# Second attention's first unit placed beside the last shared units of the first feed-forward

## The chip, the core and the metric

The kernel runs on one core of one Trainium2 chip. A core has five engines with a queue of instructions each: PE (TensorE, matrix products; its weight loads are listed as PEld), DVE (VectorE), ACT (ScalarE), POOL (GpSimd) and SP (SyncE, which here issues DMAs). Each engine takes its own instructions strictly in the order of its queue, and engines wait for each other by semaphores. The metric is the device time of one execution in microseconds (us).

## The reference

Two layers in float32 on x of 4 x 1024 rows of 256 numbers, that is 32 row tiles of 128 rows (NT = 32):

```
x = x + windowed_attention(layernorm(x))       # 16 heads, window 64
x = x + moe(layernorm(x))                      # first feed-forward
x = x + attention(layernorm(x))                # 16 heads over all keys, then a layernorm
x = x + expert_choice(layernorm(x))            # second feed-forward, sinkhorn gates
```

The first feed-forward has eight routed experts, of which each row uses its best two, and two shared experts whose mean every row gets. An expert is silu(x w1 + b1) * (x w2 + b2), times w3, plus b3, with 512 hidden columns. In the second attention 64 rows of 256 numbers are reread as the 1024 positions of one head (the reference reshapes to (B * H, S, D) without a transpose), so that a unit of rows can be attended to without the others. The second feed-forward takes sinkhorn gates and lets each expert choose 128 of 1024 rows.

## The kernel before

The rows lie in SBUF for the whole kernel, as tiles x_t[0] to x_t[31]. Four tiles make a unit (UT = 4, NU = 8). A scheduler in the language keeps the order in which instructions are written as a start, reorders each engine's queue by its own estimates, and puts in the waits that data and reuse of memory ask for. Pools hand out SBUF; a tile that takes over memory of an earlier one waits for that one's last reader.

*First feed-forward.* normalise writes the normed rows xn_kept of each tile and their transposes xnT. The gate chooses two experts for each row; 64 scatters (L840, one for each tile and choice, on POOL) write rows to xs_d in DRAM sorted by expert. Beside them run the shared experts: shared(E, u) for all eight units, then shared(E + 1, u) for u = 0 and 1. One shared(e, u) is 32 matmuls of 128x512 at L657, a Silu at L665 on ACT and a product at L666 on DVE for each of four groups f, then 32 matmuls at L674 and four updates of x_t at L683. Then 31 blocks of sorted rows go through their experts (L876 transposes, L893 and L920 matmuls), with expert weights from a pool f0_e of three buffers, and their results are written to ys_d. After the blocks the second shared expert's weights are loaded again (load_expert) and shared(E + 1, u) runs for u = 2 to 7. After these in the program come 64 gathers (L947, indirect DMAs on POOL, three buffers yr0): each fetches the rows of one tile and one choice from ys_d, and DVE adds them, weighted, to x_t[i] (L953). note(i) then takes mean and variance of tile i on DVE (L137, L138); roots takes the square root on ACT and the reciprocal on DVE (L143, L144).

*Constants of the second feed-forward* follow (L965 to L1000): two iotas, the zero fill of rank_d and of the last row of y_d by six DMAs on POOL.

*Second attention.* Weights and biases are loaded (w_raw, b_raw on SP; bv_b and rows_b on POOL), two top_st tiles and minus are filled by memsets on POOL (L1308 to L1313). project(u) makes, for a unit, normed rows xn (L1325, on POOL), their transposes (L1335), q and k (L1345 matmuls, L1356 and L1357 split them in two parts) and writes these to DRAM as halves. load(p) reads them back as q_st and k_st, the stack for head pair group p, into a ring of RING stacks. values(u) makes v_t. maxima_step computes scores once (L1423 on PE, two matmuls) and their row maxima (L1430 on DVE). AHEAD = 12 steps of these, two halves each, are issued before the main loop; the loop of NP * KT + 1 = 257 steps then, for each step, computes scores less the row maximum (L1465), exponentials (L1473 on ACT), sums with v (L1480), and the maxima 12 steps ahead. Between them some() runs small jobs, twice a step: generators that yield when they have given enough work for one turn. put_out (L1513 to L1526) adds the bias bo on POOL (L1525) and the projection on DVE; finish makes the last norm on POOL (L1553 to L1558).

*Ranks.* When the first half of the batch has been gated, the generator ranks() issues 16 scatters on POOL (L1591) that write a row's place to rank_d; it yields 0 after each, so that they may all be issued in one turn. choose_steps later reads rank_d and makes key.

Of the kernel before, what the change touches and what calls it, by code (L numbers as in the profile page):

```python
# [18 lines left out]
P = 128  # L19
# [10 lines left out]
E = 8  # L30
# [9 lines left out]
def two_layers(  # L40
# [464 lines left out]

    with ExitStack() as lc:  # L510
        wpool = lc.enter_context(tc.tile_pool(name="f0_w", bufs=1))
        epool = lc.enter_context(tc.tile_pool(name="f0_e", bufs=3))
        pool = lc.enter_context(tc.tile_pool(name="f0", bufs=2))
        xnT = wpool.tile([P, 2, NT * P], F32, name="xnT_f0")
        dram = lc.enter_context(tc.tile_pool(name="f0_d", bufs=1, space=bass.MemoryType.DRAM))
# [21 lines left out]
        for k in range(2):  # L537
            t = pool.tile([P, D], F32, tag="yr0", name="sb3_k", bufs=3)
            nc.gpsimd.dma_start(out=t, in_=sb3[k].partition_broadcast(P))
            if k == 0:  # L540
                nc.gpsimd.tensor_scalar(sb3_b, t, 0.5, None, ALU.mult)
            else:
                nc.gpsimd.tensor_scalar(t, t, 0.5, None, ALU.mult)
                nc.gpsimd.tensor_tensor(sb3_b, sb3_b, t, ALU.add)
# [90 lines left out]
        def kept_rows(i: int):  # L635
            xn_all.append(wpool.tile([P, D], F32, name=f"xn_kept{i}"))
            return xn_all[i]

        def load_expert(w1, w2, w3):
# [8 lines left out]
        def shared(e: int, weights, u: int):  # L648
# [3 lines left out]
            glu = pool.tile([P, NF, UN], F32, tag="glu", name="glu")  # L652
            for f in range(NF):
# [10 lines left out]
                act = pool.tile([P, UN], F32, tag="act", name="act", bufs=3)  # L664
# [3 lines left out]
                )  # L668
            for jp in range(UT // 2):
# [11 lines left out]
                for jj in range(2):  # L681
# [8 lines left out]
                    )  # L690

# [6 lines left out]
        first = load_expert(sw1[0], sw2[0], sw3[0])  # L698
# [154 lines left out]
        second = load_expert(sw1[1], sw2[1], sw3[1])  # L853
# [3 lines left out]

        for t0, nt, n in order:
# [4 lines left out]
                *(w[bass.ds(e, 1)].rearrange("e k f -> (e k) f") for w in (rw1, rw2, rw3))  # L863
            )
            b3_t = pool.tile([P, 1, D], F32, tag="b3", name="b3_t")
# [3 lines left out]
            xb = pool.tile([P, 2, D], F32, tag="xb", name="xb", bufs=2)  # L869
# [11 lines left out]
            xbT = pool.tile([P, 2, BT], F32, tag="xbT", name="xbT")  # L881
# [45 lines left out]
            yb = pool.tile([P, 2, D], F32, tag="yb", name="yb")  # L927
# [11 lines left out]
        second = load_expert(sw1[1], sw2[1], sw3[1])  # L939
        for u in range(2, NU):  # L940
            shared(E + 1, second, u)


        for i in range(NT):
            for k in range(2):
                yr = pool.tile([P, D], F32, tag="yr0", name="yr0", bufs=3)
                nc.gpsimd.indirect_dma_start(  # L947
                    out=yr[:, :],
                    out_offset=None,
                    in_=ys_d[:, :],  # L950
                    in_offset=bass.IndirectOffsetOnAxis(ap=slots[k][:, i : i + 1], axis=0),
                )
                nc.vector.scalar_tensor_tensor(  # L953
                    x_t[i], yr, weight[k][:, i, :], x_t[i], ALU.mult, ALU.add
                )
            note(i)

    fc = ctx.enter_context(ExitStack())
    fpool = fc.enter_context(tc.tile_pool(name="f1_w", bufs=1))
    gpool = fc.enter_context(tc.tile_pool(name="f1", bufs=2))
    fdram = fc.enter_context(tc.tile_pool(name="f1_d", bufs=1, space=bass.MemoryType.DRAM))
    GB = 2  # L965
    GE = GB * E
    TB = S // P
    GT = GB * TB

    gw1 = fpool.tile([P, 2, E], F32, name="gw1")  # L970
    nc.sync.dma_start(out=gw1, in_=gate1_w.rearrange("(k p) e -> p k e", p=P))

    number_i = fpool.tile([P, E], I32, name="number_i")
    nc.gpsimd.iota(number_i, pattern=[[1, E]], base=0, channel_multiplier=0)
    number = fpool.tile([P, 1, E], F32, name="number")
    nc.vector.tensor_copy(number[:, 0, :], number_i)
    first_slot = fpool.tile([P, 1, E], F32, name="first_slot")
    nc.vector.tensor_scalar(first_slot, number, float(CAP), -1.0, ALU.mult, ALU.add)

    place1_i = fpool.tile([P, 1], I32, name="place1_i")  # L980
    nc.gpsimd.iota(place1_i, pattern=[[0, 1]], base=1, channel_multiplier=1)
    place1 = fpool.tile([P, 1], F32, name="place1")
    nc.vector.tensor_copy(place1, place1_i)
    gates = fpool.tile([P, NT, E], F32, name="gates")

    xn_d = [fdram.tile([S, D], F32, name=f"xn_d{b}") for b in range(NB)]

    y_d = [fdram.tile([E * CAP + 1, D], F32, name=f"y_d{b}") for b in range(NB)]

    rank_d = [fdram.tile([S * E, 1], F32, name=f"rank_d{b}") for b in range(GB)]  # L990
    none = fpool.tile([P, S * E // P], F32, name="none")
    nc.gpsimd.memset(none, 0.0)
    for b in range(GB):
        nc.gpsimd.dma_start(out=rank_d[b].rearrange("(p n) o -> p (n o)", p=P), in_=none)
    for b in range(NB):
        nc.gpsimd.dma_start(
# [790 lines left out]
```

## Time and profile before

| | us |
|---|---|
| median of 3 runs | 2609.26 |
| lowest, highest | 2599.96, 2613.25 |
| time of the profiled execution | 2548.45 |
| its span in the profile | 2546.3 |
| mean granted clock of PE in it | 0.94 |
| last block's last matmul (L920) | 1144.8 |
| last shared unit ends on PE | 1275.4 |
| last gather starts | 1278.8 |
| first maxima matmul (L1423) | 1317.5 |
| first exponential (L1473) | 1354.8 |
| 16 rank scatters (L1591) | 2309.2 to 2329.2 |

The profile is of one execution. Its rows give for each engine the busy time; times of day are us from the start of the span. "PEclk" is the share of its full clock that PE was granted. A row of waits says which engine and instruction waited for which: us in total, how often, the longest. "A to B" rows give busy us of each engine in that stretch with the number of instructions in brackets. The median of the runs is 2.4% above the profiled execution; parts of the time are read in the profiled execution.

### The profile page before, as it was taken

What the parts mean: (1) busy time and instruction counts of PE and PEld (TensorE: products, weight loads), DVE (VectorE), ACT (ScalarE), POOL (GpSimd) and SP (SyncE); (2) the same over time, 40 slices, a digit from 0 to 9 for tenths busy, and PEclk for the clock granted to TensorE, in tenths of its full rate; (3) what the DMA queues carried; (4) which work ended last, traced back from release to release, by engine and by line L of the source; (5) the groups of instructions that cost most, each with busy time, mean ns of one, the idle gap of its engine ahead of it and who ended that gap; (6) DMA issues with size and microseconds to landing.
All of it is one profiled execution on the core that took longest, in us unless ns stands there. A gap on an engine that the chain in (4) does not pass through costs nothing. (4 is left out here: it accounts for less than half of the span.)

```text
span 2546.3 us, 42216 instructions
## 1 busy us (share of the span) xinstructions
PE 2291.9 (90%) x16844; PEld 1361.5 (53%) x16844; DVE 1398.2 (55%) x2294; ACT 980.1 (38%) x1350; POOL 639.7 (25%) x742
## 2 busy tenths in 40 slices
PE   6999999799999999998948999999999999997534
PEld 3666666566578888885524444444444444443322
DVE  6445445524322222225446777677777898984293
ACT  1333333312112222221103666565666565665311
POOL 2333333510710000005330021212222212124355
PEclk8988999899999999999968999999999999998667
DMA  3000000320346667652152121213121312100134
GB/s 93 18 10 10 11 12 10 125 77 3 131 160 212 205 206 230 206 172 75 50 118 68 35 68 44 68 44 68 44 68 43 68 44 67 44 19 11 54 120 132
DMA packets 201535, 206.46 MB, mean 81 GB/s; under 512 B 89224, under 2 KB 161544, under 8 KB 201340
## 3 DMA queue, kind: packets, MB, share of 16 engines
q1 hardware_dynamic: 178732, 163.24, 22.4%
q0 software_dynamic: 11792, 30.18, 4.0%
q10 hardware_dynamic: 10816, 10.36, 1.2%
q8 instruction: 133, 2.18, 0.4%
q14 instruction: 62, 0.51, 0.1%
HBM read 142.28 MB, written 56.96 MB: 78 GB/s over the span
## 5 line engine op out<-in xcount | busy, mean ns | idle before, releaser
L1430 DVE TENSOR_REDUCE tops<-two 128x2 f32<-128x1024 f32 x512 | 619.4, 1218 | 128.1 <-PE two L1423 126.0
L1473 ACT ACTIVATE pT<-two 128x1024 f32<-128x1024 f32 x512 | 523.0, 1024 | 331.3 <-PE two L1465 326.6
L1480 PE MATMUL acc<-pT,v_t 128*32 128x256 f32 x4096 | 346.3, 398 | 5.3 <-ACT pT L1473 5.3
L1465 PE MATMUL two<-q_st,k_st 64*128 64x512 f32 x1024 | 262.0, 504 | 31.8 <-DVE tops L1430 19.5
L893 PE MATMUL two<-xbT,w_t 128*128 128x256 f32 (+1 forms) x1280 | 257.9, 356 | 1.3 <-ACT xbT L882 0.7
L1423 PE MATMUL two<-k_st,q_st 64*128 64x512 f32 x1024 | 233.2, 422 | 20.2 <-DMA k_st<-halves 9.4
L893 PEld LDWEIGHTS two<-xbT,w_t 128*128 128x128 f32 x1280 | 222.7, 190 | 31.1 <-ACT xbT L882 5.1
L657 PE MATMUL two<-xnT_f,w_t 128*128 128x512 f32 x512 | 230.4, 601 | 5.6 <-DVE glu L666 5.6
L1465 PEld LDWEIGHTS two<-q_st,k_st 64*128 64x128 f32 x1024 | 97.4, 185 | 224.8 <-issue 128.2
L1465 PE MATMUL two<-top_st,minus 64*128 64x512 f32 x1024 | 209.2, 402 | 0.0
L909 DVE SCALAR_TENSOR_TENSOR glu_b<-two,b_blk,act_b 128x256 f32<-128x256 f32 (+1 forms) x160 | 72.6, 454 | 228.7 <-ACT act_b L903 228.7
L903 ACT ACTIVATE act_b<-two,b_blk 128x256 f32<-128x256 f32 (+1 forms) x160 | 71.9, 450 | 310.9 <-PE two L893 159.5
L947 POOL DMA_INDIRECT yr<-ys_d,slot x64 | 61.2, 956 | 499.5 <-DMA ys_d<-yb 433.0
L1480 PEld LDWEIGHTS acc<-pT,v_t 128*32 128x32 f32 x4096 | 87.0, 109 | 169.6 <-issue 147.7
L657 PEld LDWEIGHTS two<-xnT_f,w_t 128*128 128x128 f32 x512 | 96.4, 193 | 114.1 <-issue 105.8
L1423 PEld LDWEIGHTS two<-k_st,q_st 64*128 64x128 f32 x1024 | 108.1, 192 | 92.2 <-DVE tops L1430 28.8
L920 PE MATMUL acc<-w_t,glu_b 128*128 128x256 f32 x568 | 148.5, 390 | 8.3 <-DVE glu_b L909 4.0
L355 DVE TENSOR_REDUCE top<-two 128x4 f32<-128x768 f32 (+1 forms) x128 | 112.5, 919 | 69.4 <-PE two L329 69.4
L381 POOL TENSOR_SCALAR_AFFINE_SELECT pT<-pT 128x1024 f32<-128x1024 f32 x64 | 70.2, 1097 | 305.8 <-ACT pT L378 300.4
L378 ACT ACTIVATE pT<-two 128x768 f32<-128x768 f32 (+1 forms) x128 | 93.7, 783 | 123.0 <-PE two L329 122.6
L665 ACT ACTIVATE act<-two,bT 128x512 f32<-128x512 f32 x64 | 44.0, 687 | 242.2 <-PE two L657 239.5
L1525 POOL TENSOR_TENSOR y<-y,rows_b 128x256 f32<-128x256 f32 x32 | 23.4, 733 | 431.6 <-DVE y L1522 431.6
(320 smaller groups left out, 3185.1 us busy)
## 6 DMA issues: line engine op xcount, KB each, us to landing
w_t<-in_L_ffn_rw_dram SPq DMA_DIRECT2D x120, 512.0 KB
halves<-split SPq DMA_DIRECT2D x64, 256.0 KB
q_st<-halves SPq DMA_DIRECT2D x128, 128.0 KB
k_st<-halves SPq DMA_DIRECT2D x256, 64.0 KB
xb<-xs_d SPq DMA_DIRECT2D x31, 256.0 KB
ys_d<-yb ACTq DMA_DIRECT2D x31, 256.0 KB
xs_d<-zeros SPq DMA_DIRECT2D x5, 1536.0 KB
b_t<-in_L_ffn_rb_dram SPq DMA_DIRECT2D x40, 128.0 KB
```

Source lines behind the costliest of these rows:

```text
L355: nc.vector.tensor_reduce(tops[i][:, 2 * ab : 2 * ab + 2, 2 * gp : 2 * gp + 2], scs[ab], AX.X, ALU.max)
L378: nc.scalar.activation(pt[:, 2 * ab : 2 * ab + 2, :, :n], scs[ab], AF.Exp)
L657: mm(ps[:, n * 512 : (n + 1) * 512], lhsT=w_t[:, kc, f * P : (f + 1) * P], rhs=xnT[:, kc, cols], start=(kc == 0), stop=(kc == 1),)
L893: mm(ps[:, m * 512 + ff * cols : m * 512 + (ff + 1) * cols], lhsT=w_t[:, kc, f * P : (f + 1) * P], rhs=xbT[:, kc, :cols], start=(kc == 0), ...
L903: nc.scalar.activation(act[:, :cols], ps[:, ff * cols : (ff + 1) * cols], AF.Silu, bias=b_blk[0][:, f, n : n + 1],)
L909: nc.vector.scalar_tensor_tensor(glu[:, f, :cols], ps[:, 512 + ff * cols : 512 + (ff + 1) * cols], b_blk[1][:, f, n : n + 1], act[:, :cols ...
L920: mm(ps[:, a * D : (a + 1) * D], lhsT=glu[:, f, a * P : (a + 1) * P], rhs=w3_t[:, f, :], start=(f == 0), stop=(f == NF - 1),)
L1423: mm(sc[:, hh], lhsT=q_st[rows, j * P : (j + 1) * P], rhs=k_st[rows, kk * 512 : (kk + 1) * 512], start=True, stop=True,)
L1430: newest["vector"] = nc.vector.tensor_reduce(tops[:, :, j, kk], sc, AX.X, ALU.max).ins
L1465: mm(sc[:, hh * 512 : (hh + 1) * 512], lhsT=minus[rows] if top else k_st[rows, k * P : (k + 1) * P], rhs=(top_ring[p % 2] if top else q_st ...
L1473: newest["scalar"] = nc.scalar.activation(pt, sc, AF.Exp).ins
L1480: newest["tensor"] = mm(oT_ps[32 * r : 32 * r + 32, hh * D : (hh + 1) * D], lhsT=vals[n // HU][:, n % HU, k, :], rhs=pts[r // 2][:, hh * 5 ...
```

## The change

1. The pool and the constants of the second feed-forward (L965 to L1000, with the zero fill of rank_d and y_d, and ones1) are written ahead of the first feed-forward. The constant number of that stage is called expert_no.
2. The shared experts' weights get a pool of their own, f0_s, with two buffers; the second is loaded once. xn_kept lies in a pool f0_k that is closed before the blocks; the pools of the blocks, f0_e and f0_b, take memory from there on. The gathers have seven buffers (yr0) in place of three.
3. What the second attention needs for its first unit (weights, two stacks of q and k, one top_st, minus, xnT, split) is taken from the other end of SBUF (side="right"), so that it can live beside the first feed-forward's pools. The rest (further stacks, the second top_st, wo_t, rows_b, v_t and others) is taken after the first feed-forward's pools are closed. The fills are on DVE, bv_b and rows_b are loaded by SP, project(0)'s xn is on DVE (L1317 after).
4. shared becomes a generator shared_steps with six steps (four groups f, two pairs of tiles). Gathers are issued by fetch(i): tiles 0 to 3 ahead of shared(E + 1, 2), then two tiles for each step. A generator stacks (roots of tiles 0 to 3, project(0), load(0), load(1), 24 halves of maxima) advances by one yield for each step. After unit 7 the pools are closed, and values(0), roots of tiles 4 to 31, project(1) and load(2) follow, then the main loop.
5. ranks(): each scatter is made to depend on the newest exponential, and wait(2) stands between scatters.

Line numbers in the changed kernel: those of shared are L707, L715, L716, L725 and L734; of project L1317, L1337, L1348 and L1349; the gathers and their updates L1649 and L1655; the maxima L1415 and L1422; scores, exponentials and sums L1457, L1465 and L1472; the rank scatters L1583; y + bo L1517.

```diff
+    ffn0 = ExitStack()
     with ExitStack() as lc:
-        epool = lc.enter_context(tc.tile_pool(name="f0_e", bufs=3))
+        spool = ffn0.enter_context(tc.tile_pool(name="f0_s", bufs=2))
+        kept = ExitStack()
+        kpool = kept.enter_context(tc.tile_pool(name="f0_k", bufs=1))
...
+        kept.close()
+        epool = lc.enter_context(tc.tile_pool(name="f0_e", bufs=3))
+        bpool = lc.enter_context(tc.tile_pool(name="f0_b", bufs=2))
         for t0, nt, n in order:
...
-        second = load_expert(sw1[1], sw2[1], sw3[1])
-        for u in range(2, NU):
-            shared(E + 1, second, u)
-        for i in range(NT):
-            for k in range(2):
-                yr = pool.tile([P, D], F32, tag="yr0", name="yr0", bufs=3)
...
-            note(i)
...
-        wpool = lc.enter_context(tc.tile_pool(name="a1_w", bufs=1))
+        wpool = lc.enter_context(tc.tile_pool(name="a1_w", bufs=1, side="right"))
+        apool = lc.enter_context(tc.tile_pool(name="a1_e", bufs=2, side="right"))
...
-                    nc.gpsimd.tensor_scalar(
+                    (nc.gpsimd if u else nc.vector).tensor_scalar(
                         xn, x_t[i], mv_all[:, i, 0:1], rstd_all[:, i : i + 1],
...
-                yield 0
+                tc.add_manual_dep(
+                    sc.ins,
+                    newest["scalar"].name,
...
+                yield from wait(2)
...
-        roots(0, UT)
-        for job in (project(0), values(0)):
-            for _ in job:
-                pass
+        def fetch(i: int):
+            for k in range(2):
+                yr = f0pool.tile([P, D], F32, tag="yr0", name="yr0", bufs=7)
+                nc.gpsimd.indirect_dma_start(
...
+        def stacks():
+            roots(0, UT)
+            yield
+            for did in project(0):
+                if did:
+                    yield
+            for p in range(2):
+                load(p)
+            for _ in range(4):
+                yield
+            for m in range(AHEAD):
+                for kk in range(2):
+                    maxima_step(m, kk)
+                    yield
+
+        for i in range(UT):
+            fetch(i)
+            note(i)
+        fetched = iter(range(UT, NT))
+        beside = stacks()
+        for u in range(2, NU):
+            for _ in shared_steps(E + 1, second, u):
+                for i in (next(fetched, None), next(fetched, None)):
+                    if i is not None:
+                        fetch(i)
+                        if i < 2 * UT:
+                            note(i)
+                next(beside, None)
+            for i in range(u * UT, (u + 1) * UT):
+                note(i)
+        for _ in beside:
+            pass
+        ffn0.close()
...
+        for _ in values(0):
+            pass
         roots(UT, NT)
         projects.append(project(1))
-        for p in range(3):
-            load(p)
-        for m in range(AHEAD):
-            for kk in range(2):
-                maxima_step(m, kk)
+        load(2)
```

## The prediction

> **What bounds the kernel now.** I read the page first: TensorE is busy for 2291.9 of 2546.3 us, so time can only be won where it stands idle or runs at half clock.
>
> ```profile
> span 2546.3 us, 42216 instructions
> PE 2291.9 (90%) x16844; PEld 1361.5 (53%) x16844; DVE 1398.2 (55%) x2294; ACT 980.1 (38%) x1350; POOL 639.7 (25%) x742
> PEclk8988999899999999999968999999999999998667
> ```
>
> The chain of waits shows only the last few us, so I cut the span into stretches. Columns: stretch and length, then busy us of PE, PEld, DVE, ACT and POOL, granted clock, DMA share, GB/s.
>
> ```profile
> 1230.00:1250.00 20.00, 20.00 (x62) 11.41 (x62) 10.12 (x24) 2.75 (x4) 7.66 (x8) 1.00 0.19 53
> 1270.00:1280.00 10.00, 5.36 (x25) 4.39 (x24) 5.48 (x15) 0.38 (x1) 4.78 (x5) 0.95 0.18 52
> 1280.00:1290.00 10.00, 0.00 (x0) 0.00 (x0) 3.48 (x12) 0.32 (x1) 7.47 (x16) 0.50 0.51 135
> 1290.00:1300.00 10.00, 6.62 (x14) 3.28 (x15) 1.74 (x2) 1.17 (x2) 8.77 (x11) 0.52 0.17 40
> 1300.00:1310.00 10.00, 8.79 (x76) 5.35 (x74) 3.98 (x6) 2.75 (x4) 0.00 (x0) 1.00 0.68 141
> 1310.00:1320.00 10.00, 1.61 (x3) 0.82 (x3) 0.32 (x1) 0.00 (x0) 0.00 (x0) 0.66 0.95 199
> 1330.00:1340.00 10.00, 7.30 (x20) 3.07 (x18) 9.97 (x10) 0.00 (x0) 0.00 (x0) 0.50 0.06 10
> 1350.00:1360.00 10.00, 7.20 (x36) 3.13 (x34) 3.45 (x4) 3.81 (x4) 0.00 (x0) 0.50 0.03 8
> 2320.00:2330.00 10.00, 0.00 (x0) 0.00 (x0) 0.00 (x0) 0.28 (x1) 7.82 (x9) 0.68 0.07 4
> ```
>
> The last shared units (1192 to 1275.4) fill PE at full clock. Then comes the seam: the last gathers, the second attention's weights and constants, project(0), the stack loads, 24 maxima bound by DVE, at half clock. The first exponential starts at 1354.8, the fourth at 1359.05; from there a step takes about 4.0 us. The seam is 1275.4 to 1359, some 83 us. The second hole is 2320 to 2330. The waits of PE name both:
>
> ```profile
> PE two L1465 <- DVE tops L1430: 19.5, 12, 11.7
> PE misc L1282 <- POOL top_st L1308: 15.5, 1, 15.5
> PE two L1423 <- DMA k_st<-halves: 9.4, 2, 7.9
> ```
>
> The gathers, which the change moves in among the shared units, by their line:
>
> ```profile
> L947 POOL DMA_INDIRECT yr<-ys_d,slot x64: 940/957/1037, 1148.2 to 1278.8; - x64
>   DVE x L953: 47.4, 8
> DMA to landing us min/median/max: 2.6/2.7/3.8
> ```
>
> POOL stood 47.4 us waiting for the three yr buffers; with seven that wait is small and a gather can follow each 0.96 + 0.30 issue = 1.26 us: 64 take 81 us, from 1148.2 to 1229, and the last lands by 1232.
>
> **What the seam could give.** PE work moved in front: project(0) with its transposes about 10 us at full clock, 24 maxima pairs at 0.40 us = 10 us (0.79 at half). So of 83 us some 20 are moved, not removed, and about 8 stay after the last unit (first scores, the wait for exp, a table load of 1.28 us). Ideal gain: 83 - 20 - 8 = 55 us.
>
> **What holds it back.** DVE works in order, and the changed order puts each gather's update (L1655, 0.48 us) ahead of things that PE waits for. I walked DVE and PE through it with before's durations. The last block's PE work ends at 1144.8, its ys_d write at 1148.2. The weights' raw tiles lie in memory of the last blocks, so they can load only from about 1145, and land at 1148 to 1154 (as before: 3.3 us from 1283.24 to use); PE stalls some 3 us on the bias transpose. The n-th gather lands at 1148.2 + 1.26(n-1) + 2.8. xn of tiles 0 and 1 (now on DVE, L1317) stands behind the gathers 15 and 16: 1170, not 1161 when x3 is complete; xn of tiles 2 and 3 behind 20: 1176. The transposes stand ahead of unit 2's L725 in PE's order, so PE idles about 10 us (1160 to 1170). project(0)'s matmuls run to 1191, its second split to 1200; halves and stack loads (8.1 and about 7 us in the seam) land by 1215, well before the first maxima at about 1232. Unit 3's glu, f = 0, stands behind gather 50 (1214; PE idles 1205 to 1214), f = 2 behind 61, f = 3 behind 64 (1232). Unit 3 then ends at about 1240, where before it ended at 1192.4: 47 us have gone into the cover, 20 of them moved PE work. From there nothing waits on a gather: four units at 20.75 = 83, 21 maxima at 0.43 = 9, 1 for waits: 1333. Scores at once, first exp about 1335.5, two table loads and the square root (2 x 1.28 + 0.3, the roots of tiles 4 to 31 lie here) in between, fourth exp 1341.5. Gain of the seam: 1359 - 1341.5 = **17.5 us**. load(2) starts at 1333 and is needed at about 1350 (landing took 12 us for two stacks): hidden. project(1) goes into the main loop as before. values(0) and wo_t are small and lie beside the first steps. The memsets, two of 1.86 us and more on POOL before, go to DVE, beside the last block and unit 2; uncovered they would cost 2 to 4. Five small loads (bv, gamma, beta, bo: 1.84 + 0.64 + 0.56 + 0.54 us of POOL) go to SP at some 0.4 each; bv's two stand ahead of the halves, which have 17 us to spare.
>
> [...] If every gather lost one update's 0.48 us, 64 would take 112 us, unit 3 would end at 1271, and the seam's gain be lost (-13). The row says otherwise: gathers beside updates last 957 ns, at most 1037. I take the row. [...] 1290 to 1300 at 0.52 after the gap, and 0.50 throughout 1330 to 1360 with PE 7 us in 10 busy. By the rows a gap may cost 5 us: 10 for two. Part is hidden, since PE waits for gathers anyway up to 1232; I add nothing and put 0 to 10 in the range.
>
> **Start of the first feed-forward.** Six DMAs, two iotas and two memsets of the later stage now stand ahead of its own on POOL (1.17 + 2.13 us for the DMAs, 4 in all). They push the gate bias to about 489.7 (needed near 491) and the zero fill of xs_d by 3 to 4 us (needed only by scatters from 634). The reciprocal of the norm, 486.55 because it stood behind casts of POOL's iotas, is now ahead of them: up to 2.1 earlier. I take **-1**, range -2 to +2.
>
> **Block stage.** The expert weights take the memory of the kept rows, so the first loads wait for the last scatter (714.3, landed 717), where before one expert was fetched at 636. At 200 to 269 GB/s its 1.5 MB and xb are there by 726; PE has shared work until 729. Cost 0, range 0 to 4; if the cover were gone, 8. The second shared weights are loaded once instead of twice: a hidden 1.5 MB saved.
>
> **Ranks.** L1591's 16 scatters stood back to back on POOL (2309 to 2329.2) with y + bo (L1525) behind them; DVE waited 14.3 us for that, the tops' reductions behind it, PE 11.7 us, then some 10 us at 0.64 clock cost 3. Spaced by two half steps (4 us) each, they let one scatter at most (1.26 us) ahead of L1525: -14. Each adds a wait of POOL for a recent exp; behind it stand other POOL jobs, at most some us late. In return the last scatter moves from 2329 to the last exps at about 2380 (before's clock), lands 2.1 later, its read 3 later: 2385.8; DVE's key chain, hidden before, stands ahead of x31's update (2386.64 before). That costs 2 to 4. Net **-11**, range -14 to -4.
>
> **Sum** on the profiled execution (2548.45 us, 2.15 beside its span): -17.5 - 1 - 11 = -29.5, 2519. The median of the runs lies 60.8 above it; the profile does not say where, so I subtract the same: 2609.26 - 29.5 = **2580**.
>
> **Rivals.** (A) The gathers don't hold PE: DVE takes updates early enough, clock full. Seam 55: -67, 2542. For: DVE is 60% busy there. Against: the order above. Chance 0.14. (B) Slower. One mechanism, DVE's order among gathers, projection and shared units: an update behind a glu or a split that waits for PE holds its yr buffer, POOL stops, and the gathers again last from 1148 to 1281 as in before. Then unit 3 ends at 1289, the fourth exp comes at 1390: +31.5 - 12 = +20, 2629. It decides from the point where the gathers end after about 1261, 30 us later than walked. For: 47.4 us of just such waits in before. Against: seven buffers. Chance 0.1. (C) The pace does not give: the hole of 2320 is filled but the tail takes it back; seam 17.5 alone or less: -18 to -8, about 2596. Chance 0.18. Main case -45 to -18: 0.58.
>
> **Numbers.** About 0.5% (13 us) is what a measurement can tell from no change. Faster by more: the main case, A and half of C: 0.81. Within: the rest of C and 0.02 of B: 0.11. Slower: 0.08. The range 2545 to 2603 takes the main case, C and part of A.
>
> **What would show it.** Right: fourth exp about 17 us earlier; unit 3's end near 1240; gathers 81 to 90 us long; PE gaps near 1160 and 1205 with reductions of clock; no PE hole at the ranks; L1591 spread over 60 us. Wrong: gathers over 110 us long (B), shared units without gaps (A), a new PE gap before the blocks or a longer end after the last exp (C).

## The result and the profile after

The changed kernel takes 2594.26 us (median of 15 runs, 2589.91 to 2605.3) against 2609.26 (15 runs, 2599.96 to 2616.95): ratio 0.9949, interval 0.9934 to 0.9964, that is 13.3 us faster by the ratio (9 to 17); the two medians lie 15.0 apart. Forecast were 29.5. The direction was right and 2594 lies in the stated range, but more than half of the gain is missing.

First the head of the changed kernel's profile: the span, the busy time of each engine, and PE and its granted clock in 40 slices of 65 us.

```profile
span 2602.1 us, 42203 instructions
PE 2294.8 (88%) x16844; PEld 1360.5 (52%) x16844; DVE 1394.5 (54%) x2303; ACT 982.2 (38%) x1351; POOL 633.2 (24%) x728
PE   6999999899289999998589999999999999998534
PEclk8998999899689999999699999999999999999667
```

PE does as much as before (16844 matmuls, 2294.8 us busy against 2291.9), but the span is 55.8 us *longer* than in the profile of before, although the timed runs are shorter. Two slices tell of it: the "2" in the eleventh (650 to 715), which before's profile does not have in this place, and "85" in the nineteenth and twentieth (1171 to 1301). The first is not the change's doing, as will be shown. So the two profiled executions can't be subtracted from each other; timed runs are compared on one chip, and stage lengths inside each trace.

The waits of PE in the changed kernel, beside those shown of before (which engine and line waited for what: us in all, times, longest):

```profile
PE misc L725 <- DVE glu L716: 43.5, 4, 21.2
...
PE two L707 <- DVE glu L716: 17.8, 2, 16.8
PE two L707 <- issue: 12.8, 3, 10.9
```

Before's three waits of the seam and the ranks (for top_st, the tops and k_st) are gone from the head of the list. In their place PE waits for the gated product of shared units (L716), and for "issue", that is for nothing that the profile names. A row of "issue" can hide a wait, though: its longest, 10.9 us, ends at 1298.63, and DVE's product L716 ended at 1298.58 (its line is shown below).

**Stage lengths.** To place the gain, six moments are taken from every trace: the start of the last block matmul (L920, L975 after), the end of unit 3 and of unit 7 (the last update of x), the start of the fourth and of the last exponential, and the span's end. "Seam" is the way from the last block matmul to the fourth exponential, "blocks" the way from the first shared matmul to the first matmul of that line. Each row is a single execution. The last six rows belong to the experiments below. All in us.

| kernel | blocks | unit 3 done | units 4-7 | to 4th exp | seam | loop | tail |
|---|---|---|---|---|---|---|---|
| before, profile shown | 243.0 | +48.8 | +83.0 | +82.8 | 214.6 | 1018.2 | 169.1 |
| before, again | 244.5 | +50.7 | +83.0 | +84.2 | 217.9 | 1018.6 | 169.5 |
| before, third | 242.8 | +50.0 | +83.0 | +84.5 | 217.5 | 1013.6 | 168.9 |
| after, again | 242.9 | +98.7 | +99.1 | +8.5 | 206.3 | 1000.6 | 170.4 |
| after, third | 242.4 | +100.9 | +100.8 | +8.5 | 210.2 | 999.5 | 171.7 |
| **after, profile of the result** | **308.2** | **+107.5** | +99.1 | +8.5 | 215.1 | 1000.5 | 171.4 |
| **after, fourth** | **311.5** | **+109.3** | +100.8 | +8.5 | 218.6 | 1000.4 | 171.9 |
| **pace only** | **309.1** | +49.2 | +82.9 | +84.2 | 216.3 | 1003.2 | 172.9 |
| no scatters | 244.5 | +99.2 | +99.1 | +8.5 | 206.8 | 1000.4 | 174.6 |
| no pace | 242.8 | +99.5 | +99.1 | +8.5 | 207.1 | 1012.4 | 168.8 |
| late stacks | 242.5 | +78.8 | +82.7 | +65.8 | 227.3 | 1000.5 | 170.1 |
| no gathers | 242.2 | +50.8 | +100.7 | +8.5 | 160.0 | 1003.4 | 173.5 |
| one per step | 242.3 | +88.8 | +107.8 | +8.5 | 205.1 | 1002.8 | 170.4 |
| paced gathers | 242.0 | +72.4 | +104.9 | +8.6 | 185.9 | 1004.5 | 170.0 |

The seam has the forecast's shape, and its last part the forecast's number: 8.5 us from unit 7 to the fourth exponential. But unit 3 comes 99 to 109 us after the blocks (forecast 95), and units 4 to 7 take 99 to 101 (forecast 93). The loop is 13 to 19 us shorter than before's. And three executions (bold) lose 65 to 69 us before the blocks.

**The hole before the blocks.** In windows of the changed kernel's profile (columns as in the prediction):

```profile
630.00:650.00 20.00, 19.51 (x61) 11.02 (x60) 19.14 (x61) 2.75 (x4) 8.48 (x9) 1.00 0.13 48
...
690.00:710.00 20.00, 1.22 (x2) 0.50 (x2) 0.75 (x1) 0.69 (x1) 15.22 (x16) 0.50 0.29 105
```

From about 661 to 730 PE's rows show next to nothing (11.30, 6.26, 1.22 and 2.07 us busy in the four windows between 650 and 730), while POOL issues the 64 scatters of rows (639 to 720, 16 in 20 us). The activations of the shared experts in the same trace, and PE's rows beside them:

```profile
698.94 0.69 ACT L715 ACTIVATE act<-two,bT 128x512 f32<-128x512 f32 x1 [21.72 <-issue]
721.33 0.69 ACT L715 ACTIVATE act<-two,bT 128x512 f32<-128x512 f32 x1 [21.70 <-remote]
729.10 0.69 ACT L715 ACTIVATE act<-two,bT 128x512 f32<-128x512 f32 x1 [7.08 <-remote]
```

```profile
650.83 10.46 PE L707 MATMUL two<-xnT_f,w_t 128*128 128x512 f32 x24
678.06 5.83 PE L707 MATMUL two<-xnT_f,w_t 128*128 128x512 f32 x8 [16.76 <-DVE glu L716]
```

The idle time before each stands in brackets. One activation needs eight matmuls of L707 with eight weight loads. It comes every 22.4 us here (676.53 was the one before), against every 3.43 us without the hole; once the scatters end (720) it takes 7.77. PE's rows do not show eight slow matmuls for each: 24 of them, three groups, start within 650.83 to 661.3 as fast as ever. Yet the activations that need these groups start at 676.53, 698.94 and 721.33, the first of them 22 us after the eighth matmul's row. The starts are recorded and the ends of matmuls are modelled, so either PE finishes its matmuls late, with starts that run ahead, or ACT is told late; these rows do not tell which. The waits "for glu L716: 43.5" above are this hole: PE waits for DVE's product, the product for the activation, and the activation for a group of matmuls whose rows are long past.

### The profile page after: what moved, and what is told of

Same layout as the page of the kernel before. It is cut to its first block, busy times and chain, and to the rows that moved or that the text cites. A ratio compares the mean times of both kernels' runs of the same rounds, so it can differ in the third digit from the quotient of the medians.

```text
span 2602.1 us, 42203 instructions
## 1 busy us (share of the span) xinstructions
PE 2294.8 (88%) x16844; PEld 1360.5 (52%) x16844; DVE 1394.5 (54%) x2303; ACT 982.2 (38%) x1351; POOL 633.2 (24%) x728
## 4 chain that ended last, share of the span: by engine, by line
PE 32%; DVE 11%; issue 3%; ACT 2%; POOL 1%; DMA 1%; SPq 0%; POOLq 0%; ACTq 0%; DVEq 0%
PE two L1457 9%; PE acc L1472 8%; DVE tops L1422 5%; PE two L1415 4%; PE two L707 2%; PE two L1337 2%; DVE top_i L1097 1%; PE misc L1377 1%; ACT pT L1465 1%; DVE top_v L1095 1%; DVE cur L1101 1%; PE misc L1511 1%; PE acc L725 1%; PE misc L725 1%; PE misc L1034 1%
## 5 line engine op out<-in xcount | busy, mean ns | idle before, releaser
L1422 DVE TENSOR_REDUCE tops<-two 128x2 f32<-128x1024 f32 x512 | 620.9, 1218 | 137.3 <-PE two L1415 135.2
L1465 ACT ACTIVATE pT<-two 128x1024 f32<-128x1024 f32 x512 | 523.6, 1025 | 303.1 <-PE two L1457 295.3
L1472 PE MATMUL acc<-pT,v_t 128*32 128x256 f32 x4096 | 341.7, 394 | 5.6 <-ACT pT L1465 5.6
L1457 PE MATMUL two<-q_st,k_st 64*128 64x512 f32 x1024 | 259.5, 499 | 18.4 <-ACT pT L1465 11.5
L707 PE MATMUL two<-xnT_f,w_t 128*128 128x512 f32 x512 | 242.8, 622 | 32.6 <-DVE glu L716 17.8
L1415 PE MATMUL two<-k_st,q_st 64*128 64x512 f32 x1024 | 223.6, 405 | 2.4 <-DVE tops L1422 0.9
L1457 PE MATMUL two<-top_st,minus 64*128 64x512 f32 x1024 | 206.8, 396 | 0.0
L1457 PEld LDWEIGHTS two<-q_st,k_st 64*128 64x128 f32 x1024 | 96.8, 184 | 208.1 <-issue 126.4
L1649 POOL DMA_INDIRECT yr<-ys_d,slot x64 | 62.7, 980 | 527.2 <-DMA w_raw<-in_L_attn_wk_dram 499.7
L707 PEld LDWEIGHTS two<-xnT_f,w_t 128*128 128x128 f32 x512 | 97.7, 198 | 145.0 <-issue 121.7
L1472 PEld LDWEIGHTS acc<-pT,v_t 128*32 128x32 f32 x4096 | 86.3, 108 | 166.1 <-issue 142.2
L715 ACT ACTIVATE act<-two,bT 128x512 f32<-128x512 f32 x64 | 44.0, 687 | 335.8 <-PE two L707 231.1
L975 PE MATMUL acc<-w_t,glu_b 128*128 128x256 f32 x568 | 148.6, 390 | 8.3 <-DVE glu_b L964 4.0
L1415 PEld LDWEIGHTS two<-k_st,q_st 64*128 64x128 f32 x1024 | 103.8, 185 | 77.1 <-ACT pT L1465 22.3
L1517 POOL TENSOR_TENSOR y<-y,rows_b 128x256 f32<-128x256 f32 x32 | 23.6, 736 | 429.6 <-DVE y L1514 429.6
```

What stands on the lines that cost most here:

```text
L707: mm(ps[:, n * 512 : (n + 1) * 512], lhsT=w_t[:, kc, f * P : (f + 1) * P], rhs=xnT[:, kc, cols], start=(kc == 0), stop=(kc == 1),)
L975: mm(ps[:, a * D : (a + 1) * D], lhsT=glu[:, f, a * P : (a + 1) * P], rhs=w3_t[:, f, :], start=(f == 0), stop=(f == NF - 1),)
L1415: mm(sc[:, hh], lhsT=q_st[rows, j * P : (j + 1) * P], rhs=k_st[rows, kk * 512 : (kk + 1) * 512], start=True, stop=True,)
L1422: newest["vector"] = nc.vector.tensor_reduce(tops[:, :, j, kk], sc, AX.X, ALU.max).ins
L1457: mm(sc[:, hh * 512 : (hh + 1) * 512], lhsT=minus[rows] if top else k_st[rows, k * P : (k + 1) * P], rhs=(top_ring[p % 2] if top else q_st ...
L1465: newest["scalar"] = nc.scalar.activation(pt, sc, AF.Exp).ins
```

## The experiments

Twelve runs were made, on four chips; those of one numbered group share the chip and the runs of the kernel before, which took 2537.84, 2538.3, 2545.04 and 2609.68 us there. Which chips the first profile and the result came from is not known. In the expectations, theory T says that PE is slowed while POOL issues indirect DMAs back to back (its "one instruction for each" is an estimate from the hole above: 16 instructions of PE, eight matmuls and eight weight loads, to one activation in 22.4 us, in which POOL issues some 18 scatters at one per 1.25 us); rival R1 says that the change makes the hole, and rival R2, the prediction's own mechanism, that DVE's order among gathers holds PE.

**1. Before, again, no scatters, no pace, late stacks** (one chip). The first question was whether the hole belongs to the change. The kernel before, as it is:

> The kernel before, unchanged, profiled once more. Theory (T): while POOL issues indirect DMAs back to back, PE completes only about one instruction for each of them; this hole of some 60 us at the scatters (640 to 730) is in most runs of both kernels and was absent from the one profiled execution of before. Then this run takes 2600 to 2615 us, and PE is idle for 50 to 65 us between 640 and 740. Rival (R1): the hole comes from the change (kept rows and expert weights in one place); then PE stays full at the scatters here and the 60 us by which the runs exceed 2548 lie elsewhere.

It took 2534.75 us (one run), not 2600 to 2615. The same scatters lie beside the same shared units, and PE does not notice. Its window from 650:

```profile
650.00:670.00 20.00, 20.00 (x63) 11.72 (x62) 3.83 (x7) 2.75 (x4) 15.12 (x17) 1.00 0.30 105
```

POOL does here exactly what it did in the hole (17 instructions, 15.12 us, 105 GB/s); what differs is PE, and with it ACT and DVE. This run alone could still mean that the change makes the hole. It did not: see pace only.

The changed kernel without the scatters of rows:

```
-        for i in range(NT):
+        for i in range(0):
             for k in range(2):
                 sc = nc.gpsimd.indirect_dma_start(
                     out=xs_d[:, :],
```

> The changed kernel with the 64 scatters of normed rows left out (the routed blocks then work on the zero fill; all matmuls stay). T: the hole at 650 to 735 goes, some 60 us: about 2534, ratio 0.97. R1 (loads that wait for the kept rows, or anything but the scatters' issue): less than 15 us.

It took 2526.96 us against 2537.84, ratio 0.9947 (0.9928 to 0.9966). No gain over the changed kernel with its scatters (0.992 and 0.990, on other chips, below) is to be seen: without the hole, the scatters show no cost. As a test of the hole it is inconclusive, since the hole was not there to be removed.

The ranks without their pace:

```
-                tc.add_manual_dep(
-                    sc.ins,
-                    newest["scalar"].name,
-...
-                yield from wait(2)
+                yield 0
```

> The changed kernel with the rank scatters back to back and without their dependence on an exponential, as before. From the two profiles the main loop is 17.7 us shorter and the tail 2.4 longer by the pacing: +15 on 2594, 2609, ratio about 1.000. The prediction's own figure gives +11, 2605. If the loop got shorter by something else: 2594.

It took 2521.18 us against 2537.84, ratio 0.9934 (0.9912 to 0.9955). Against the changed kernel's 0.992 and 0.990 on other chips that is hard to tell apart by time, but its trace shows the term: the loop is 1012.4 us instead of 1000.6 and 999.5, the tail 168.8 instead of 170.4 and 171.7. So the pace gives about 12 in the loop and costs 2 to 3 in the tail: 10 net. (On this chip itself only no scatters has the pace; its loop is 1000.4 too, but its tail is 174.6, which would leave 6.) Its windows at the ranks:

```profile
2300.00:2310.00 10.00, 0.00 (x0) 0.00 (x0) 0.27 (x1) 0.00 (x0) 7.53 (x9) 0.67 0.07 4
2310.00:2320.00 10.00, 8.66 (x53) 2.92 (x53) 7.15 (x23) 4.25 (x5) 6.86 (x8) 0.65 0.14 33
```

The hole of before is back, with 0.65 of the clock behind it. In the changed kernel run again, the scatters of ranks spread and PE goes on (windows, then the line of the scatters with its first and last start):

```profile
2310.00:2320.00 10.00, 8.17 (x74) 3.73 (x70) 1.64 (x6) 6.48 (x8) 9.49 (x12) 0.96 0.00 0
```

```profile
L1583 POOL DMA_INDIRECT rank_d<-place,at_i x16: 957/980/1102, 2288.4 to 2347.2; - x16
```

Last, the gathers left among the shared units, but all of stacks() put behind them. That takes project(0) along: its first matmul (L1337) starts at 1308.3 here, and unit 7 is done at 1304.8.

```
                         if i < 2 * UT:
                             note(i)
-                next(beside, None)
             for i in range(u * UT, (u + 1) * UT):
```

> The changed kernel with the gathers still among the shared units, but roots, project(0), the stack loads and the 24 maxima all after unit 7. If the gathers alone stretch the shared units (T, PE slowed by indirect DMAs), the cover of the seam is worth its 55 us and these come back on top: about 2640 to 2650. If instead the work put beside the units stretches them (rival R2: DVE's order of gathers, xn and glu), taking it away shortens the units by about 17 more: 2620 to 2630.

It took 2539.11 us against 2537.84, ratio 0.9998 (0.9978 to 1.0018): the whole gain of the ranks is eaten. Both expectations, set against 2609 for before, were too high (2620 to 2630 for R2 is 1.004 to 1.008, T's 1.012 and more); R2 comes nearer. The table takes the seam apart: with the gathers alone among the units, unit 3 is 28 to 30 us later than before; what follows the last unit falls by 17 to 19 only, because project(0), the stacks' way through memory (PE waits 12.3 us for k_st) and the maxima still stand behind it. PE's clock stays at 0.50 from 1320 to 1360; the first half of that:

```profile
1320.00:1340.00 20.00, 7.20 (x16) 3.08 (x16) 6.83 (x7) 0.00 (x0) 0.00 (x0) 0.50 0.85 185
```

Putting project(0), stacks and maxima beside the units then removes 57 us behind them and adds some 36 to 40 in front (20 to 22 up to unit 3, 16 to 18 in units 4 to 7). The gathers' half of the move alone makes the seam some 10 us longer than before's.

**2. After, again, before, third, no gathers, one per step** (another chip).

> The changed kernel unchanged, timed beside the kernel before once more. The run with the rank scatters back to back stood at 0.9934 of before on its chip; the pacing's loop and tail are 10.3 us shorter in the profiles, so this should stand at 0.9934 less 0.004: 0.989 to 0.990, some 27 us, if PE is not slowed during indirect DMAs there (theory T, a matter of the chip or the moment). If the chip shows that slowing, 0.995 as in the first measurement. Rival: the change is worth 15 us everywhere, ratio 0.9949.

It took 2519.53 us against 2538.3, ratio 0.9921 (0.9893 to 0.9949), and there is no hole: blocks start 242.9 us after the first shared matmul. Nor has the kernel before one on this chip:

> The kernel before, unchanged, beside the others. T: its time follows the hole at the scatters: about 2600 to 2615 with PE idle for some 60 us between 640 and 730, or about 2540 without.

It took 2540.73 us. Its seam is 217.5 us, the changed kernel's 206.3. How the 99 us up to unit 3 come about, in the changed kernel's windows there:

```profile
1157.00:1177.00 20.00, 9.14 (x19) 4.45 (x20) 11.76 (x32) 1.47 (x3) 15.12 (x17) 0.53 0.37 106
1177.00:1197.00 20.00, 18.02 (x54) 10.01 (x53) 12.08 (x29) 5.20 (x7) 15.12 (x17) 0.98 0.71 181
1197.00:1217.00 20.00, 8.15 (x12) 3.18 (x11) 8.09 (x19) 0.69 (x1) 15.24 (x16) 0.59 1.06 223
```

Two gaps of PE, where the prediction had placed them, and each with a clock of 0.5 to 0.6. Their names, from the waits of PE between 1130 and 1340:

```profile
PE misc L1327 <- DVE xn L1317: 15.6, 3, 12.1
PE two L707 <- DVE glu L716: 11.8, 1, 11.8
```

DVE is 8 to 12 us in 20 busy: it is not short of time but waits, in its own order, for gathers to land (37.8 us in all before L1655), with the rows of project(0) and the gated products behind them. The order is seen in the rows: in the two profiles of before and after, all 2294 and 2303 rows of DVE start in the order in which their lines stand in its queue; so do those of ACT (1350 and 1351) and POOL (738 and 724 with a line of the kernel), and PE's 16844 but for one pair, 3 ns apart in after. And the product that ends PE's wait of 11.8 us starts at 1211.57, behind an update (1211.17) that had waited 1.09 us for its gather.

Now the gathers and their updates left out (so the routed part of the first feed-forward is missing from x):

```
         def fetch(i: int):
 
-            for k in range(2):
+            for k in range(0):
                 yr = f0pool.tile([P, D], F32, tag="yr0", name="yr0", bufs=7)
```

> The changed kernel with the 64 gathers and their updates of x left out (the routed experts' part is missing from x). In the unslowed profiles the time from the blocks' end to unit 3's end was 99.5 us, against 49 in before; the prediction gives 20 of these 50 to moved PE work and the rest to DVE's queue of gathers. If so, without gathers unit 3 ends 65 to 75 us after the blocks, and the fourth exponential comes 25 to 30 us earlier than in the changed kernel. If the stacks' own waits hold PE (w_raw, bias, xn, splits), it stays above 90.

It took 2480.88 us (one run), 57 below before's 2538.3. The seam is 160.0 us, 55 to 58 less than before's three and 46 to 50 less than with gathers, where 25 to 30 were expected; unit 3 is done at +50.8, not at +65 to +75. PE stands full at full clock where the gaps were; the window of the first, and from 1202 to 1222 it is the same, 20.00 at 1.00:

```profile
1162.00:1182.00 20.00, 20.00 (x60) 11.21 (x59) 7.13 (x18) 4.10 (x6) 0.00 (x0) 1.00 0.83 182
```

So the "ideal gain" of 55 is there to be had, and 46 to 50 of it go with the gathers. The waits of PE say how: those for xn and glu, 33 us in the changed kernel (15.6, 11.8 and two of 5.8 together), are gone, and none over 1.9 us is left. Leaving the gathers out takes away their DMA traffic and POOL's work as well, so this run alone does not single out DVE's order; paced gathers, below, keeps both. It also gives back what gathers cost in before: there PE waited 6.4 us for products up to unit 3 (profile shown), which is part of how project(0)'s work of some 10 us could come in front and unit 3 still be as early as before. Units 4 to 7, which no gather touches, take 100.7 here too, so the 99 to 101 are no work of the gathers.

Then the gathers at half the rate, one tile for each step of a unit instead of two, so that they would spread over 32 steps:

```
             for _ in shared_steps(E + 1, second, u):
-                for i in (next(fetched, None), next(fetched, None)):
-                    if i is not None:
-                        fetch(i)
-                        if i < 2 * UT:
-                            note(i)
+                i = next(fetched, None)
+                if i is not None:
+                    fetch(i)
+                    got = i + 1
+                while noted < min(done, got):
+                    note(noted)
+                    noted += 1
                 next(beside, None)
```

> The changed kernel with one tile's gathers (two) for each shared step in place of two tiles', so that POOL (1.26 us a gather) is never behind and DVE's updates rarely wait; means taken as soon as a tile has both parts. If the gathers in DVE's order are what holds units 2 and 3, these shorten by 10 to 25 us, and the kernel is that much faster than the changed one: ratio 0.980 to 0.985. If the stacks' own waits hold them, it equals the changed kernel.

It took 2518.19 us, ratio 0.9902 (0.987 to 0.9935); the same as the changed kernel there, where 0.980 to 0.985 were expected. It did not spread the gathers, so it decides nothing between the two readings: POOL has nothing else to do and runs ahead. The line of the gathers in this kernel, and a wait of PE that is new:

```profile
L1649 POOL DMA_INDIRECT yr<-ys_d,slot x64: 942/946/2290, 1142.9 to 1232.2; - x64
...
PE two L707 <- DVE tops L1422: 11.3, 1, 11.3
```

89 us instead of 81, hardly any spreading. Unit 3 came 10 us earlier and units 4 to 7 took 9 more: the wait for the tops was 1.9 in the changed kernel.

**3. Paced gathers, after, third** (a third chip). One per step as above, and from tile 4 on each gather waits, as the ranks do, for the activation of the step that it belongs to (acted, not shown here, keeps the newest one; the change of one per step is in it too):

```
+                if i >= UT:
+                    tc.add_manual_dep(
+                        ga.ins,
+                        acted["scalar"].name,
+                        mybir.DependencyInfo(
+                            mybir.DependencyClass.Sync, mybir.DependencyReason.DATA
+                        ),
+                        reason="pace",
+                    )
```

> The changed kernel with one tile's gathers for each shared step, and each gather (from tile 4 on) made to depend on the activation of that step, so that POOL really spreads them (in the run with one tile for each step they still went out back to back, since nothing held them) and the scheduler puts the updates behind the products of later steps. Without gathers unit 3 ended 50.8 us after the blocks and the fourth exponential came 160 us after them; with all in a row 98.7 and 206.3. If the early updates in DVE's queue are the price, unit 3 ends at 55 to 70 and the fourth exponential comes at 165 to 180: 26 to 41 us faster than the changed kernel, ratio to before 0.976 to 0.982. If the gathers' DMA traffic or POOL itself is the price, it stays near 200 and the ratio near 0.992.

It took 2500.08 us (2495.27 to 2507.36) against 2545.04, ratio 0.9829 (0.9801 to 0.9858), and beats both kernels. It falls just short of what was expected on all three counts (unit 3 at 55 to 70, seam 165 to 180, ratio 0.976 to 0.982). The changed one on the same chip:

> The changed kernel once more beside the others, for the ratio: 0.992 (0.989 to 0.995) where PE is not slowed at the scatters and before takes about 2538; 0.995 and a hole between 640 and 740 where before takes about 2609.

It took 2522.55 us, ratio 0.9903 (0.987 to 0.9936). With the paced gathers unit 3 is done 72.4 us after the blocks instead of 100.9, and the seam is 185.9 instead of 210.2 us. The gathers in this kernel, the one wait of PE for DVE's products in its seam, and two of its windows:

```profile
L1653 POOL DMA_INDIRECT yr<-ys_d,slot x64: 940/946/2262, 1139.6 to 1281.6; - x64
...
PE acc L729 <- DVE glu L720: 14.8, 6, 9.2
```

```profile
1155.00:1175.00 20.00, 15.44 (x39) 8.38 (x40) 12.21 (x35) 3.18 (x6) 8.69 (x9) 0.68 0.42 105
1215.00:1235.00 20.00, 19.66 (x64) 10.59 (x62) 13.41 (x21) 2.06 (x3) 11.35 (x12) 1.00 0.25 72
```

They last 142 us, longer than before the change (131), and PE is nearly full in the second window. *Slower* gathers are better here. All 64 gathers, their traffic and their updates are still there; what fell is PE's wait for xn and glu, from 34.4 us in the changed kernel on this chip (16.1, 12.5 and 5.8) to 14.8. So the pace shows 24 of the 46 to 50 us to be a matter of when gathers go out and where their updates stand; the other 22 to 26 are bound to the gathers too, but how they divide between the products still waited for (14.8), the clock (0.68 in the first window) and the rest is open.

**4. Pace only, after, fourth** (a fourth chip: the kernel before takes 2609.68 us here). The kernel before with nothing but the pace of the ranks:

```
                 tc.add_to_no_dep_group("to_ranks", sc.ins)
-                yield 0
+
+                tc.add_manual_dep(
+                    sc.ins,
+                    newest["scalar"].name,
+...
+                yield from wait(2)
```

> The kernel before with the pacing of the rank scatters alone. The prediction's step gives -11 (loop less 11.7 + 3 of half clock, tail plus 2 to 4); undoing the pacing in the changed kernel lengthened loop and tail by 10.3. So -10 to -12: ratio 0.9955 to 0.996. If the pace only moves the wait to the tail (the prediction's rival C), 0.999 to 1.000. On a chip where PE is slowed during the scatters of rows its profile shows a hole between 640 and 740 in this kernel too.

It took 2599.63 us, ratio 0.9962 (0.9945 to 0.9978): the pace alone is worth 9.9 us (5.7 to 14.4). And here, in before's own order of the seam, is the hole at the scatters (windows of pace only):

```profile
650.00:670.00 20.00, 0.28 (x1) 0.00 (x0) 0.76 (x2) 0.00 (x0) 15.33 (x16) 0.56 0.30 105
...
690.00:710.00 20.00, 1.22 (x2) 0.50 (x2) 0.75 (x1) 0.69 (x1) 14.76 (x16) 0.50 0.29 101
```

The activations come at 670.01, 692.41 and 714.81, 22.4 us apart as well. The blocks start 309.1 us after the first shared matmul, as in the changed kernel (308.2).

> The changed kernel beside it: seam (blocks' end to fourth exponential) 206 to 210 us where PE is not slowed at indirect DMAs (before: 215 to 218), 215 where it is, as in its first profile.

One run: 2586.43 us, 23 below before's median. Hole 311.5, unit 3 at +109.3, as in the result's own profile. So the hole does not come from the change: it follows the chip, or the time at which that chip ran, which cannot be told apart with one group of runs for each. Pace only and the changed kernel have it here, and before, the changed kernel and no pace do not have it on the others. The times agree with that: all 50 executions on this chip, before's 27 among them, took 2586 to 2622 us, and before's 50 on the other three took 2528 to 2555.

## Why the prediction was wrong in its size

**The offset of 60.8 us that "the profile does not say where".** It is, by all signs, the hole at the scatters. The profile of before shown has blocks 243 us after the first shared matmul; pace only, on a chip where before's median is 2609.68, has 309: 66 us. (Before itself was not profiled with the hole.) The forecast was right to carry the offset over unchanged, as both kernels have it (308.2 and 311.5 after). But it stood for a behaviour that the change then met a second time.

**Seam, -17.5: the step that failed.** The mechanism was right, DVE's order among gathers, projection and shared units; the sizes in the walk were not, and one cost stood in it at nothing. On chips without the hole it gave -9: before's three seams average 216.7, the changed kernel's two 208.2, or 207.2 with those of no pace and one per step. The walk gave 196.7 from the last block matmul to the fourth exponential (1341.5 less 1144.8), so 11 us were missing in it. Its shape was as walked; these terms were mis-sized:

- *Unit 3 at +95* was +98.7 to +100.9. The two gaps were forecast at 10 and 9 us and are 12.1 (15.6 with two short ones) and 11.8: together 8 more, of which 4 to 6 reach the end. The clock at 0.53 and 0.59 in these stretches was put in the range only ("I add nothing"). Of the 47 us that the walk puts into the cover up to unit 3, 20 were to be moved PE work; but only project(0) and five matmuls of the maxima stand there, and without gathers that work came at no loss (+50.8). Nearly all of the 47 was the gathers.
- *21 maxima at 0.43 = 9* were 22 pairs at 0.64 = 14.1. The PE timeline of the profiled execution shows why; a pair, the shared step's eight matmuls, and the next pair:

```profile
1401.62 0.51 PE L1415 MATMUL two<-k_st,q_st 64*128 64x512 f32 x2
1402.06 3.70 PE L707 MATMUL two<-xnT_f,w_t 128*128 128x512 f32 x8
1405.69 0.50 PE L1415 MATMUL two<-k_st,q_st 64*128 64x512 f32 x2
```

  From pair to pair 4.07 us, where the step alone took 3.43 in before. The pair itself occupies 0.44 of that; the rest is the eight matmuls after it, 3.63 from start to next start. What the pair costs between others is 0.64 here, where its own place in the order is 0.44 long; why the eight behind it take 0.2 us more is open. With a wait of 1.9 for the tops (L1422; forecast 1) units 4 to 7 took 16 to 18 over their 83, forecast 10.
- *From unit 7 to the fourth exponential* the 8.5 us are right by luck: the first exponential came 1.2 us after the last update in the changed kernel run again (forecast 2.5), the fourth 7.3 after the first (forecast 6.0, though before's 4.25 and the 2.86 for tables and root add to 7.1).
- *Where the hole is* (in the result's own profile too) the gain of the seam is nil: 215.1 and 218.6 against pace only's 216.3. This is the cost that the walk had at nothing: PE slowed beside the gathers. The 9 us more than elsewhere lie in the part up to unit 3 (+107.5, +109.3). There the changed kernel's gathers stand back to back as the scatters do, and PE crawls; its timeline, and a line of DVE:

```profile
1265.21 0.38 PE L725 MATMUL misc<-w_t,glu 128*128 128x256 f32 x1 [2.24 <-issue]
...
1297.83 0.75 DVE L716 SCALAR_TENSOR_TENSOR glu<-two,bT,act 128x512 f32<-128x512 f32 x1
1298.63 6.15 PE L707 MATMUL two<-xnT_f,w_t 128*128 128x512 f32 x8 [10.90 <-issue]
```

  Four single matmuls, 2.1 to 2.8 us apart and waiting for nothing that the profile shows: from the first of these 16 matmuls (1260.22) to the next group (1274.33) it takes 14.1 us, where the changed kernel run again needs 3.5 (1182.66 to 1186.11). The pause of 10.9 us is another thing: it ends with DVE's product, which stands behind updates of gathers, and is the second gap of the walk. In pace only, where three buffers spread the gathers over 131 us (1209 to 1340), unit 3 is not late (+49.2). So there the gathers in quick succession seem to cost twice: once in DVE's order, once in PE itself. That the second is the same thing as the hole at the scatters is argued from the likeness of the two, not shown. If it is, PE's slow rows with no wait behind them that the profile shows speak for the first reading above: PE itself is late.

For gathers beside updates I had taken the row of 957 ns, and that held: the gathers' median is 946 to 947 ns beside the same updates, and unit 3 without the hole is at +99 to +101, where the prediction's estimate, with an update's 0.48 us lost at every gather, had it at +126 (1271 less 1144.8).

**Rival A** (no hold, -67) is refuted by the same traces; no gathers shows what it would have been. **Rival B** (buffers stop POOL) did not occur: the gathers take 89 to 90 us where the hole is, 81 to 82 elsewhere. **Rival C** (the tail takes the pace back) did not either, though 2 to 4 us of tail were given back, as forecast.

**Ranks, -11:** right. Measured -9.9 alone (5.7 to 14.4), 6 to 10 as the difference of no pace.

**Start of the first feed-forward, -1:** about 0, as two terms cancel. From the last matmul of the first attention to the first shared matmul it is 11.9 us before and 12.1 in the changed kernel (start to start). The normed rows do come 2.1 us earlier, as forecast (PE waits 2.6 for xn_kept instead of 4.7). But the gate bias, forecast in time, lands too late behind the six DMAs: DVE waits 2.5 us for it (L639), and PE 2.0 to 2.4 us for DVE. **Block stage, 0:** right; blocks begin 242.4 to 242.9 us after the first shared matmul with the change, 242.8 to 244.5 without.

**The sum.** Where the hole is: seam +0.6 (216.9, the mean of 215.1 and 218.6, less 216.3) and ranks -9.9: -9 against -13 measured (9 to 17). Elsewhere: -9 and -9.9: -19 against 0.9921 and 0.9903, that is -20 and -25. What is left over is within what single traces differ by (loops of the paced kernels: 999.5 to 1004.5). The forecast of -29.5 failed in the seam: some 5 in the gaps, some 7 in units 4 to 7, and, with the hole, 9 in the crawl of PE.

Left open: what holds PE, or the word that its matmuls are done, while POOL issues indirect DMAs back to back on that chip; that the scatters are the cause is read from their times alone. Taking the scatters out, or pacing them, was not tried there.

## What to carry to other kernels

Work moved in front of a wait was paid for here at the engine that it passes through: DVE, with its rows in the order of its queue, waited 37.8 us for gathers to land, and PE 33 us for DVE. So put an update in the queue where its data will have landed, and if the issuing engine runs ahead (64 gathers in 81 us), pace it; here slower gathers won 22 us over faster ones (0.9829 against 0.9903). A cover is worth only what its own order allows: measure it by leaving the suspect out (160.0 against 206 us of seam), and then by moving it, since leaving it out takes its other costs along. And if the profiled execution lies 60 us beside the median, find the hole first; it may be a behaviour that the change meets again. In such a hole, look at which rows are late: here the matmuls that ACT waited for had their rows 22 us before.

## What was not expected of the hardware

On one of four chips, and with both kernels, a group of eight matmuls with their eight weight loads was answered by its activation only every 22.4 us (instead of 3.43) for as long as POOL issued scatters at one per 1.25 us, while the matmuls' own rows still stood 0.43 us apart. The last activation before it ends 5 us after the first scatter (644 and 639; 633 and 628 in pace only), and it ends about with the last scatter (719 and 708); DMA share (0.30) and bandwidth (105 GB/s) were the same as on a chip where PE ran full. It costs 65 to 69 of 2600 us, whatever the change.

The granted clock stayed at 0.50 for at least 40 us (1320 to 1360 in late stacks) with PE busy in 7.2 and 16.2 of 20 us. In the profile of before it was 0.50 from 1320 to 1360 too, with PE busy in 6.97 to 7.30 of each 10 us, and 0.95 in the next 10, with PE busy in 9.91; what brought it back is not shown.
